# Expert stage of a conv-attention kernel: expert outputs on four rows, 21 weight buffers, outputs gathered group by group, and half of the tokens turned back earlier

## The chip, the cores and the metric

The kernel runs on one core of a Trainium2 chip. Its time is the device time of one execution in microseconds (us); three runs of the kernel before gave 2455.71, 2457.27 and 2457.47, median 2457.27. The profile is of one more execution. Engines: PE multiplies matrices (PEld is its weight load), DVE and ACT are the vector and the scalar engine, POOL a general one, SP issues transfers; ACT can issue transfers too, from its own queue.

## The reference

Four images of 128 channels and 64 x 64 pixels (4096 tokens each) pass a convolution with attention over all pixels (layer 0), then a causal attention over tokens with eight heads, then a layer of 64 experts. In that last part each expert picks its own tokens. In short:

```python
t = t + L1_attn(ln_t(t))                      # B=4, 4096 tokens, D=128
x = ln_t(t)
logits = x @ gate_w.T + gate_b                # B, 4096, E=64
probs = softmax(logits, axis=1)               # over tokens
vals, idx = top_k(probs.transpose(0, 2, 1), 8)      # 8 tokens for each expert and image
pooled = einsum('bked,bke->bed', gathered_x, topv)  # weighted sum of the 8 tokens
h = concat([pooled.transpose(1, 0, 2), 1])
h = gelu(einsum('ebd,edh->ebh', h, weight1))        # 128 -> 512, exact gelu
out = einsum('ebh,eho->ebo', concat([h, 1]), weight2)  # 512 -> 128
outputs[b, idx] += out * topv                 # back to the picked tokens
t = t + outputs                               # then to B, C, H, W
```

An expert thus sees four vectors, one for each image, and has 512 KB of weights.

## The kernel before

Layer 0 and the attention take the first 2288.66 us of the span and are the same in both kernels but for the matmuls with the means and a copy of them on POOL, named below. The tokens `t` stay in SBUF, 128 tokens by 128 channels in each of 128 chunks. A block is 512 tokens (four chunks); there are 32 blocks (`NB`), eight for each image.

**The loop.** `loop()` runs the attention over the 32 blocks. The order of its instructions on PE is as written (`manual_schedule`). Two blocks behind the attention it computes gate logits (`gate_stats`, `gate_norm`, `gate_turn`, `gate_logits`) into `lgs[p]`, where p = 0 holds images 0 and 1 on the two halves of the partitions, and p = 1 images 2 and 3. Once images 0 and 1 are complete, eight rounds of the loop each also pool one of their blocks: `pick_mark` marks each expert's chosen tokens, `pick_exp` takes the exponentials on ACT, `pick_keep` sets all others to zero (so `lgs` becomes a sparse weight for each expert and token), `pick_turn` transposes it and multiplies by the tokens' reciprocal deviation, and `pick_sum` (line 1007) multiplies it with the tokens `t`, and a second time with their means, a matmul of a single column. `pick_add` adds the block's sum to `total`.

**After the loop** the order on each engine is planned by the framework from its own estimates of instruction times and arrivals; an engine then runs its list in order. A tile that is written again waits for its earlier readers. There are four parts:

- Gate of the last block, then `select(1)` (the 8 largest logits of each expert).
- Pooling of images 2 and 3: for each of eight blocks `pick` (mark, exp, keep), `pick_turn`, `pick_sum` into the PSUM tile `pp`. `pool_tokens` subtracts the mean, scales, and transposes into `pooled`, which holds 32 columns for each expert: four images and 28 zeros.
- Experts, in 16 groups of four. `first(g)` (line 1168) multiplies `pooled` with each expert's first weights into `ph`; the four experts use four different column strips of PE and write 32 rows each. ACT copies `ph` to `hr`, `turn` transposes it (`htr`, line 1180), DVE adds the bias (`hs`), ACT applies Gelu. `second(g)` (line 1195) multiplies with the second weights into `po`; DVE adds `po` to `outs`. Weights come on SP's queue into 15 buffers (`load_expert`, line 1117); a buffer is loaded again once `second` has read it. Between groups `back(n)` (line 1209) turns two blocks of `t` back to channels by tokens: four transposes, and one copy on DVE or ACT. One of `lgs`'s blocks is scaled on ACT for each group.
- End: 16 transfers gather the four used rows of `outs` into `eo` (line 1233; half on SP, half on ACT). For each block and image a matmul `sct` (line 1249) spreads the outputs to the tokens, DVE adds it to `t` (line 1256), and SP writes two blocks at a time to memory (line 1259).

PSUM tiles of the tag `kv` after the loop (transposes, logits, `sct`) share four buffers.

Of the kernel before, what the change touches and what calls it, by code (L numbers as in the profile page):

```python
# [18 lines left out]
def conv_attn_hybrid_kernel(  # L19
# [90 lines left out]
    def load_layer1(upper):  # L110
        nc.sync.dma_start(out=wks, in_=wkt.rearrange("d (h e) -> d h e", h=NH))
        nc.sync.dma_start(out=wvs, in_=wvt)

# [554 lines left out]
    NW = 15  # L668

    def layer1(pre, ready):  # L670

        with ExitStack() as kept, ExitStack() as l1:
# [226 lines left out]
            total = lgp.tile([P, B // 2, C + 1], F32, tag="total", name=f"{pre}total")  # L899
# [7 lines left out]
            def gate_norm(n, engine):  # L907
# [9 lines left out]
                nc.gpsimd.tensor_copy(mv1[:, bass.ts(n, CPB), :], gmv[n])  # L917
# [9 lines left out]
            def gate_logits(n, ps):  # L927
# [7 lines left out]
                nc.scalar.activation(lg, pl[rows_b, :], AF.Identity, bias=gbs[rows_b, :])  # L935
# [24 lines left out]
            def pick_mark(p, k):  # L960

                left = gp.tile([P, BLK], F32, tag="left", name=f"{pre}left_{p}_{k}")
# [21 lines left out]
            def pick(p, k):  # L984
                pick_mark(p, k)
                pick_exp(p, k)
                pick_keep(p, k)

# [13 lines left out]
            def pick_sum(p, k, pp, start, stop):  # L1002
                for c in range(CPB):
                    for z in range(2):
                        at = (2 * p + z) * NCH + k * CPB + c
                        for to, what in ((slice(0, C), t[:, at, :]), (slice(C, C + 1), mv1[:, at, 0:1])):
                            nc.tensor.matmul(  # L1007
                                pp[z * E : (z + 1) * E, to], cts[p, k][:, c, z, :], what,
                                start=start and c == 0, stop=stop and c == CPB - 1,
                                skip_group_check=True,  # L1010
                            )

            def pick_add(p, k):
                pp = ps_kv.tile([P, BLK], F32, tag="kv", name=f"{pre}pp_{p}_{k}")[:, : C + 1]
                pick_sum(p, k, pp, True, True)
                if k == 0:
                    nc.vector.tensor_copy(total[:, p, :], pp)
                else:
                    nc.vector.tensor_add(total[:, p, :], total[:, p, :], pp)
# [9 lines left out]
            def loop():  # L1029
# [3 lines left out]
                for n in range(NB):  # L1033
# [18 lines left out]
                    with ExitStack() as order:  # L1052
# [3 lines left out]
                        if 0 <= k0 < NBLK:  # L1056
                            order.enter_context(tc.issue_after(pick_mark(0, k0)))
# [46 lines left out]
            fwp = pool("fw", NW)  # L1104
# [3 lines left out]
            ps_h = pool("l2h", 2, space=PSUM)  # L1108
# [4 lines left out]
            def load_expert(e):  # L1113
                if e >= E:
                    return
                w = fwp.tile([P, FH + FC * C], F32, tag="fw", name=f"{pre}fw_{e}")
# [3 lines left out]

            outs = fo.tile([P, EG, C], F32, tag="outs", name=f"{pre}outs")
            for u in range(QG):
                nc.sync.dma_start(
# [200 lines left out]
```

## Time and profile before

| what | us |
|---|---|
| median of three runs | 2457.27 |
| profiled execution | 2455.56 |
| its span, first to last instruction | 2453.8 |
| end of the loop (`t` written, line 888) | 2288.66 |
| first mark of images 2 and 3 (line 964) | 2300.07 |
| first expert matmul (line 1168) | 2327.50 |
| first `sct` matmul (line 1249) | 2421.56 |
| end of the span | 2453.8 |

Times in the trace count from the first instruction. In a row of the timeline or of the chain the first number is the start and the second the length of what follows; `x4` says how many instructions the row holds. A row of the waits gives who waited for whom: us in total, times, longest. A row of a stage gives its stretch and length, the busy time of PE, PEld, DVE, ACT and POOL with their instruction counts, PE's granted clock (1.00 is full), the DMA engines' mean busy share, and GB/s. A busy PE counts matmuls in flight, whose ends are modelled.

### The profile page before, as it was taken

The numbers are of one execution on the slowest core, as the hardware profiler recorded it, in microseconds if no ns is written. First come the engines' busy times: TensorE is split into PE (matmuls) and PEld (weight loads), VectorE is DVE, ScalarE is ACT, GpSimd is POOL, SyncE is SP. The second block draws the span as 40 slices with busy tenths as digits, with TensorE's granted clock in tenths as the row PEclk, the third lists the DMA queues.
The fourth block names the chain that finished last, engine by engine and source line by source line (L and its number), as shares of the span: only waits on it lengthen the run. The fifth ranks groups of instructions, "written<-read, shape, count | busy, mean of one in ns | idle before, by whom it ended". The sixth has DMA issues, their size and how long they took to land.

```text
span 2453.8 us, 46279 instructions
## 1 busy us (share of the span) xinstructions
PE 2374.9 (97%) x19732; PEld 1584.1 (65%) x19732; DVE 1490.7 (61%) x2619; ACT 1218.0 (50%) x1624; POOL 308.2 (13%) x370
## 2 busy tenths in 40 slices
PE   6999999999999999999999998999999999999797
PEld 3567777677677677777877764555555556555543
DVE  6666666666656666555555556666666766666524
ACT  4454444444443544434434345666666666665341
POOL 0000000000000000000000003333333333334000
PEclk9999999999999999999999999999999999999898
DMA  2200020001200000200000001212121211121495
GB/s 75 79 22 16 20 61 1 18 11 24 65 5 1 22 18 14 61 5 1 1 1 1 1 1 36 54 37 53 37 51 40 48 43 37 37 53 37 165 358 202
DMA packets 60583, 111.08 MB, mean 45 GB/s; under 512 B 10192, under 2 KB 35408, under 8 KB 60240
## 3 DMA queue, kind: packets, MB, share of 16 engines
q1 hardware_dynamic: 58560, 106.53, 14.9%
q8 instruction: 156, 2.56, 0.4%
q10 hardware_dynamic: 1808, 1.51, 0.2%
q14 instruction: 59, 0.48, 0.1%
HBM read 86.38 MB, written 8.91 MB: 39 GB/s over the span
## 4 chain that ended last, share of the span: by engine, by line
PE 93%; DVE 4%; ACT 2%; issue 1%; DMA 0%; SPq 0%; DVEq 0%; ACTq 0%
PE av L510 35%; PE sc L485 18%; PE pk L722 9%; PE pv L840 9%; PE po L876 4%; PE pt L856 2%; PE ps L741 2%; PE ph L1168 1%; PE po L883 1%; PE otr L549 1%; PE pl L931 1%; PE pp L1007 1%; PE pe L427 1%; PE pa L452 1%; PE po L1195 1%; PE otr L1209 1%
## 5 line engine op out<-in xcount | busy, mean ns | idle before, releaser
L510 PE MATMUL av<-pr,am 64*128 64x512 f32 x4096 | 1050.7, 592 | 0.7 <-ACT pr L489 0.7
L489 ACT ACTIVATE pr<-sc 128x1024 f32<-128x1024 f32 x512 | 523.0, 1022 | 671.8 <-PE sc L485 603.0
L492 DVE TENSOR_TENSOR acc<-acc,pr 128x1024 f32<-128x1024 f32 x480 | 586.5, 1222 | 443.7 <-ACT pr L489 443.4
L510 PEld LDWEIGHTS av<-pr,am 64*128 64x128 f32 x4096 | 637.6, 187 | 252.2 <-issue 40.2
L485 PE MATMUL sc<-e,e 64*128 64x512 f32 x2048 | 607.9, 592 | 0.0
L485 PEld LDWEIGHTS sc<-e,e 64*128 64x128 f32 x2048 | 315.5, 187 | 102.7 <-issue 20.0
L722 PE MATMUL pk<-xt,wks 128*128 128x512 f32 x512 | 242.5, 613 | 6.3 <-DVE inside L656 4.2
L840 PE MATMUL pv<-wvs,xt 128*128 128x512 f32 x512 | 226.9, 596 | 2.1 <-ACT v L844 2.1
L844 ACT ACTIVATE v<-pv 128x512 f32<-128x512 f32 x256 | 152.6, 597 | 69.7 <-PE pv L840 69.7
L724 ACT ACTIVATE ks<-pk 128x512 f32<-128x512 f32 x256 | 148.6, 597 | 61.4 <-PE pk L722 61.1
L828 DVE TENSOR_TENSOR em<-em,rb 128x1024 f32<-128x1024 f32 x64 | 80.0, 1251 | 159.9 <-DMA rb<-rd 157.3
L840 PEld LDWEIGHTS pv<-wvs,xt 128*128 128x128 f32 x512 | 97.0, 191 | 121.2 <-issue 115.9
L722 PEld LDWEIGHTS pk<-xt,wks 128*128 128x128 f32 x512 | 91.9, 192 | 113.2 <-issue 81.6
L876 PEld LDWEIGHTS po<-v,em 64*64 64x64 f32 x4096 | 111.4, 133 | 26.7 <-DVE before L866 26.7
L819 POOL TENSOR_TENSOR em<-et,mask 128x1024 f32<-128x1024 f32 x64 | 120.3, 1901 | 8.1 <-ACT et L806 8.1
L96 POOL TENSOR_SCALAR xg<-t,gmv,grs 128x128 f32<-128x128 f32 x120 | 95.3, 806 | 197.4 <-DVE grs L92 141.8
L730 POOL MEMSET ew<- 128x1024 f32 x1 | 1.0, 951 | 942.0 <-PE pa L452 942.0
L876 PE MATMUL po<-v,em 64*64 64x128 f32 x4096 | 119.2, 271 | 0.0
L778 DVE RECIPROCAL rr<-rr 128x512 f32<-128x512 f32 x32 | 107.3, 3353 | 1.1
L763 ACT ACT_TABLE_LOAD x24 | 30.8, 1283 | 118.9 <-DVE ss L762 118.9
L764 POOL COPY state<-mm 128x1 f32<-128x1 f32 x32 | 20.6, 643 | 505.4 <-DVE mm L758 505.3
L866 DVE TENSOR_TENSOR before<-before,pt 128x128 f32<-128x128 f32 x256 | 72.5, 283 | 10.0 <-PE pt L856 4.2
(169 smaller groups left out, 2147.5 us busy)
## 6 DMA issues: line engine op xcount, KB each, us to landing
rb<-rd SPq DMA_DIRECT2D x128, 256.0 KB
fw<-in_fw_dram SPq DMA_DIRECT2D x64, 512.0 KB
t<-in_xtok_dram SPq DMA_DIRECT2D x32, 256.0 KB
out_dram<-t SPq DMA_DIRECT2D x16, 512.0 KB
e<-ee SPq DMA_DIRECT2D x63, 128.0 KB
x<-in_x_dram SPq DMA_DIRECT2D x14, 512.0 KB
e<-ee SPq DMA_DIRECT2D x63, 64.0 KB
x<-in_x_dram ACTq DMA_DIRECT2D x2, 512.0 KB
```

The costliest lines, as they stand in the source:

```text
L96: i = engine.tensor_scalar(out=dst, in0=t[:, chunk, :], scalar1=mean, scalar2=rs, op0=ALU.subtract, op1=ALU.mult)
L485: nc.tensor.matmul(sc[:, u, :], e2[halves[u], p, :], e1[halves[u], :], start=True, stop=True)
L489: nc.scalar.activation(pr, sc, AF.Exp)
L492: added.append(nc.vector.tensor_add(acc, acc, pr).ins)
L510: nc.tensor.matmul(av, am[h, j, :], pr[h, u, :], start=(j == 0), stop=(j == NCH - 1))
L722: nc.tensor.matmul(pk, wks[:, h, :], xt, start=True, stop=True)
L724: nc.scalar.activation(ks, pk, AF.Silu)
L778: inverse = nc.vector.reciprocal(rr, rr).ins
L819: nc.gpsimd.tensor_tensor(em, eq.unsqueeze(2).to_broadcast([P, 2 * NH, H2]), mask.unsqueeze(1).to_broadcast([P, 2 * NH, H2]), ALU.mult,)
L840: nc.tensor.matmul(pv.rearrange("p h d -> p (h d)"), xt[:, bass.ts(2 * q + s, P)], wvs[:, bass.ts(m, BLK)], start=True, stop=True,)
L844: last = nc.scalar.activation(v[:, bass.ts(m, HPB), :], pv, AF.Silu).ins
L876: nc.tensor.matmul(po[s * H2 : (s + 1) * H2, u, q, :], aas[q][half, s, h, :], vs[2 * q + s][half, h, :], start=(q == 0 and h == 0), stop=F ...
```

## The change

- `pick_sum` no longer multiplies with the means. `pool_tokens` takes the mean of the pooled sum over its 128 channels instead, which is the same number. The copy of the means on POOL is gone, and `total` holds images 0 and 1 only; for images 2 and 3 `pool_tokens` reads `pp` itself.
- `pooled` holds four columns for each expert. The matmuls of `first` and `second` have four rows, at the first four of each strip's 32. Two `ph` tiles and one `po` tile with two halves stay for the whole stage; three matmuls with zeros clear them once. `hs` has 4 columns for each expert and chunk instead of 32.
- 21 weight buffers: 19 of the pool, and `wks` and `wvs`, the attention's projections, which nobody needs after the loop (the branch for out-of-range inputs, not taken here, loads them again).
- `outs` is gone. Each group's `po` is copied to `og` (two buffers), and four small transfers, two on SP and two on ACT, gather its rows into `eos`. The second bias is added to `eos` at the end.
- Blocks 0 to 15 (images 0 and 1) are turned back during the last gate and the pooling, with copies on ACT; the others during the experts.
- Marks run one block ahead, and `pick_turn` one block behind. Two tiny activations load the tables of Sqrt and Gelu ahead of their use.
- Outputs leave in steps of 1, 1, 2, 2, 1, 1 blocks instead of two at a time.

```diff
-    NW = 15
+    NW = 21
...
-                nc.gpsimd.tensor_copy(mv1[:, bass.ts(n, CPB), :], gmv[n])
...
-                        for to, what in ((slice(0, C), t[:, at, :]), (slice(C, C + 1), mv1[:, at, 0:1])):
-                            nc.tensor.matmul(
-                                pp[z * E : (z + 1) * E, to], cts[p, k][:, c, z, :], what,
-                                start=start and c == 0, stop=stop and c == CPB - 1,
-                                skip_group_check=True,
-                            )
+                        nc.tensor.matmul(
+                            pp[z * E : (z + 1) * E, :], cts[p, k][:, c, z, :], t[:, at, :],
+                            start=start and c == 0, stop=stop and c == CPB - 1,
+                        )
...
-            fwp = pool("fw", NW)
+            fwp = pool("fw", NW - 2)
             fo = pool("l2fo")
             fs = pool("l2fs", 2)
             ps_a = pool("l2a", 4, space=PSUM)
-            ps_h = pool("l2h", 2, space=PSUM)
+            ps_h = pool("l2h", space=PSUM)
...
+                if e % NW >= NW - 2:
+                    w = wvs if e % NW == NW - 1 else wks.rearrange("d h e -> d (h e)")
+                else:
+                    w = fwp.tile([P, FH + FC * C], F32, tag="fw", name=f"{pre}fw_{e}")
                 nc.sync.dma_start(out=w, in_=fw[e])
                 expert_weights[e] = (w[:, :FH], w[:, FH:].rearrange("p (c o) -> p c o", c=FC))
 
-
-            outs = fo.tile([P, EG, C], F32, tag="outs", name=f"{pre}outs")
-            for u in range(QG):
-                nc.sync.dma_start(
-                    out=outs[u * QW : (u + 1) * QW], in_=fb2[u : u + 1].to_broadcast([QW, EG, C])
-                )
             for e in range(NW):
                 load_expert(e)
 
-
-            pooled = fo.tile([C, E, QW], F32, tag="pooled", name=f"{pre}pooled")
-            nc.gpsimd.memset(pooled, 0.0)
-
+            eos = [fo.tile([P, C], F32, tag=f"eo{p}", name=f"{pre}eo_{p}") for p in range(B // 2)]
+            fb2s = fo.tile([P, C], F32, tag="fb2s", name=f"{pre}fb2s")
+            for z in range(2):
+                nc.scalar.dma_start(out=fb2s[z * E : (z + 1) * E, :], in_=fb2)
+
+
+            pooled = fo.tile([C, E, B], F32, tag="pooled", name=f"{pre}pooled")
+            phs = [ps_h.tile([P, FH], F32, tag=f"ph{i}", name=f"{pre}ph_{i}") for i in range(2)]
+            pos = ps_p.tile([P, 2, C], F32, tag="po", name=f"{pre}po2")
+            zeros = fo.tile([1, P], F32, tag="zeros", name=f"{pre}zeros")
+            nc.gpsimd.memset(zeros, 0.0)
+
+            def back(n, engine):
+
+                ptr = ps_a.tile([P, CPB, P], F32, tag="kv", name=f"{pre}otr_{n}")
+                at = t[:, bass.ts(n, CPB), :]
+                for c in range(CPB):
+                    nc.tensor.transpose(ptr[:, c, :], t[:, n * CPB + c, :], ident)
+                if engine is nc.scalar:
+                    nc.scalar.copy(at, ptr)
+                else:
+                    nc.vector.tensor_copy(at, ptr)
+
+
+            HB = NB // 2
+            turns = list(range(NB))
+
+            def backs(m, engine):
+                for _ in range(m):
+                    back(turns.pop(0), engine)
+
+
+            seed = fs.tile([P, 2], F32, tag="seed", name=f"{pre}seed", bufs=1)
+            with tc.issue_after(copied[pre, NB - 2]):
+                nc.scalar.activation(seed[:, 0:1], eps5, AF.Sqrt)
             gate_stats(NB - 1)
             gate_norm(NB - 1, nc.vector)
+            for to in (*phs, pos.rearrange("p i o -> p (i o)")):
+                nc.tensor.matmul(
+                    to, zeros, ones[0:1, :].to_broadcast([1, to.shape[-1]]), start=True, stop=True
+                )
+            backs(3, nc.scalar)
             gate_turn(NB - 1, ps_a)
+            backs(2, nc.scalar)
             gate_logits(NB - 1, ps_a)()
             select(1)
-            pp = ps_p.tile([P, C + 1], F32, tag="pp", name=f"{pre}pp_1")
+            backs(2, nc.scalar)
+            pp = ps_p.tile([P, C], F32, tag="pp", name=f"{pre}pp_1")
+
+            def mark(k):
+                pick_mark(1, k, fs.tile([P, BLK], F32, tag="hr", name=f"{pre}left_1_{k}"))
+
+            mark(0)
             for k in range(NBLK + 1):
                 if k < NBLK:
-                    pick(1, k)
-                    pick_turn(1, k, ps_a)
+                    exp = pick_exp(1, k)
+                if k + 1 < NBLK:
+                    mark(k + 1)
+                if k < NBLK:
+                    pick_keep(1, k)
                 if k:
+                    pick_turn(1, k - 1, ps_a)
                     pick_sum(1, k - 1, pp, k == 1, k == NBLK)
+                if turns and turns[0] < HB:
+                    backs(1, nc.scalar)
             divisors(1)

             def pool_tokens(p, sums):
+                mean = fs.tile([P, 2], F32, tag="mean", name=f"{pre}mean_{p}", bufs=1)
+                nc.vector.tensor_reduce(mean[:, 0:1], sums, AX.X, ALU.add)
+                nc.vector.tensor_scalar_mul(mean[:, 1:2], mean[:, 0:1], 1.0 / C)
                 row = fs.tile([P, C], F32, tag="row", name=f"{pre}row_{p}", bufs=1)
                 nc.vector.tensor_scalar(
-                    out=row, in0=sums[:, :C], scalar1=sums[:, C : C + 1],
+                    out=row, in0=sums, scalar1=mean[:, 1:2],
                     scalar2=rden[:, p : p + 1], op0=ALU.subtract, op1=ALU.mult,
...
-            pool_tokens(0, total[:, 0, :])
-            nc.vector.tensor_copy(total[:, 1, :], pp)
-            pool_tokens(1, total[:, 1, :])
+            pool_tokens(0, total)
+            pool_tokens(1, pp)
 
             def first(g):
 
-                ph = ps_h.tile([P, FH], F32, tag="ph", name=f"{pre}ph_{g}")
+                ph = phs[g % 2]
                 for u in range(QG):
                     e = g * QG + u
                     nc.tensor.matmul(
-                        ph[u * QW : (u + 1) * QW, :], pooled[:, e, :], expert_weights[e][0],
+                        ph[u * QW : u * QW + B, :], pooled[:, e, :], expert_weights[e][0],
                         start=True, stop=True,
...
-                hs = fs.tile([P, FC, QG, QW], F32, tag="hs", name=f"{pre}hs_{g}")
+                hs = fs.tile([P, FC, QG, B], F32, tag="hs", name=f"{pre}hs_{g}")
                 nc.vector.tensor_tensor(
-                    hs, ptr,
+                    hs, ptr[:, :, :, :B],
                     fb1s[:, bass.ts(g, QG), :].rearrange("p u c -> p c u")
-                    .unsqueeze(3).to_broadcast([P, FC, QG, QW]), ALU.add,
+                    .unsqueeze(3).to_broadcast([P, FC, QG, B]), ALU.add,
                 )
                 return hs, nc.scalar.activation(hs, hs, AF.Gelu).ins
 
             def second(g, hs):
-                po = ps_p.tile([P, C], F32, tag="po", name=f"{pre}po2_{g}")
+                po = pos[:, g % 2, :]
                 for c in range(FC):
                     for u in range(QG):
                         nc.tensor.matmul(
-                            po[u * QW : (u + 1) * QW, :], hs[:, c, u, :],
+                            po[u * QW : u * QW + B, :], hs[:, c, u, :],
                             expert_weights[g * QG + u][1][:, c, :],
                             start=(c == 0), stop=(c == FC - 1),
                         )
+                og = fs.tile([P, C], F32, tag="og", name=f"{pre}og_{g}")
+                nc.vector.tensor_copy(og, po)
                 for u in range(QG):
                     load_expert(g * QG + u + NW)
-                nc.vector.tensor_add(outs[:, g, :], outs[:, g, :], po)
-
-            def back(n):
-
-                ptr = ps_a.tile([P, CPB, P], F32, tag="kv", name=f"{pre}otr_{n}")
-                at = t[:, bass.ts(n, CPB), :]
-                for c in range(CPB):
-                    nc.tensor.transpose(ptr[:, c, :], t[:, n * CPB + c, :], ident)
-                if n % 2:
-                    nc.scalar.copy(at, ptr)
-                else:
-                    nc.vector.tensor_copy(at, ptr)
-
+                by = og.rearrange("(u w) o -> w u o", u=QG)
+                for p in range(B // 2):
+                    for z in range(2):
+                        at = z * E + g * QG
+                        (nc.scalar if p else nc.sync).dma_start(
+                            out=eos[p][at : at + QG, :], in_=by[2 * p + z]
+                        )
+
+            with tc.issue_after(exp):
+                nc.scalar.activation(seed[:, 1:2], eps5, AF.Gelu)
             hr = first(0)
             for g in range(EG):
                 hs, gelu = turn(g, hr)
                 if g + 1 < EG:
                     hr = first(g + 1)
-                for n in range(g * NB // EG, (g + 1) * NB // EG):
-                    back(n)
+                if turns:
+                    backs(1, nc.vector)
+                if turns and g % 2 and g < EG - 2:
+                    backs(1, nc.scalar)
                 p, k = g // NBLK, g % NBLK
                 probs = lgs[p][:, bass.ts(k, BLK)]
                 with tc.issue_after(gelu):
                     nc.scalar.activation(probs, probs, AF.Copy, scale=rden[:, p : p + 1])
                 second(g, hs)
-            eo = []
+            backs(len(turns), nc.vector)
+            for eo in eos:
+                nc.vector.tensor_add(eo, eo, fb2s)
+
             for p in range(B // 2):
-                eo_p = fo.tile([P, C], F32, tag=f"eo{p}", name=f"{pre}eo_{p}")
-                for z in range(2):
-                    for u in range(QG):
-                        row = u * QW + 2 * p + z
-                        (nc.scalar if p else nc.sync).dma_start(
-                            out=eo_p[z * E : (z + 1) * E, :].rearrange("(g u) o -> u g o", u=QG)[u],
-                            in_=outs[row : row + 1],
-                        )
-                eo.append(eo_p)
-
-            OB = 2
-            for p in range(B // 2):
-                for k0 in range(0, NBLK, OB):
+
+                for k0, OB in ((0, 1), (1, 1), (2, 2), (4, 2), (6, 1), (7, 1)):
```

## The prediction

> **What bounds the kernel now.** I read the page's span and chain first, then busy time by stage, then the chain in order of time inside the last stages, then the waits of SP's queue.
>
> ```profile
> span 2453.8 us, 46279 instructions
> PE 93%; DVE 4%; ACT 2%; issue 1%; DMA 0%; SPq 0%; DVEq 0%; ACTq 0%
> ...
> 2288.66:2300.07 11.41, 3.23 (x6) 1.23 (x6) 5.30 (x24) 4.13 (x5) 2.18 (x3) 0.68 1.02 318
> 2300.07:2327.50 27.43, 22.20 (x290) 18.56 (x290) 17.89 (x38) 6.51 (x16) 0.00 (x0) 0.82 0.49 195
> 2353.00:2417.60 64.60, 55.12 (x568) 28.95 (x564) 17.62 (x34) 26.06 (x44) 0.00 (x0) 1.00 0.76 295
> 2417.60:2453.80 36.20, 22.48 (x64) 9.90 (x64) 19.48 (x32) 0.00 (x0) 0.00 (x0) 0.76 0.61 238
> ```
>
> PE holds the chain, but the stages differ (columns: stretch, length, busy PE, PEld, DVE, ACT, POOL, then clock, DMA share, GB/s). The loop over token blocks ends at 2288.66. Gate and selection (11.4 us) leave PE idle. Pooling (27.4 us) runs PE at 81%, partly at a reduced clock. Experts run from 2327.50 to 2417.60, the end alone has no ACT work. All that the change touches lies in the last 165 us, but for one matmul pair inside the loop.
>
> One group of four experts, from the chain in order of time:
>
> ```profile
> 2396.07 0.66 PE htr L1180 x4
> 2396.73 0.44 PE otr L1209 x4
> 2397.16 0.98 PE ph L1168 x2
> 2398.14 0.59 PE otr L1209 x4
> 2400.66 0.65 PE ph L1168 x2
> 2401.39 0.59 ACT hr L1173
> 2402.03 0.66 PE htr L1180 x4
> ...
> SPq L1117 <- PE po L1195: 71.2, 13, 29.5
> ```
>
> A group takes 5.96 us (2396.07 to 2402.03). It is PE's written order, with one gap: the last ph ends, ACT copies hr, htr starts 0.77 us later. No wait of PE on weights appears; SP, on the contrary, waits for po to free weight buffers (last line).
>
> **The change, part by part.** Sums are made against the span, 2453.8. The profiled execution took 2455.56; the median of the runs is 2457.27, 3.5 above the span, and I carry that over.
>
> *1. Mean column of pooling, in the loop.* Each of 8 loop rounds loses 16 one-column matmuls.
>
> ```profile
> 2155.07 0.45 PE L1007 MATMUL pp<-t,ct 128*64 128x128 f32 x4
> 2155.42 0.44 PE L1007 MATMUL pp<-t,ct 128*64 128x128 f32 x4
> 2164.57 0.85 PEld L883 LDWEIGHTS po<-before,rr 128*64 128x64 f32 x16 [0.17 <-issue]
> ```
>
> A quarter of pp with its means takes 0.34 us, so 1.34 a round; 16 matmuls of the same shape without means take 0.85 (L883). Rounds with pooling last 26.7 us (t written at 1984.10 and 2010.83), rounds without 24.95, all PE: 8 x 0.49 = **-3.9**. POOL's copy of the means goes too (0.19 us, beside idle POOL: nothing).
>
> *2. Gate to first mark.* Sqrt's table load moves ahead of the wait it stood behind:
>
> ```profile
> 2290.68 1.28 ACT L91 ACT_TABLE_LOAD   x1 [6.05 <-DVE gmv L88]
> 2293.02 1.15 PE L923 MATMUL gtr<-ident,xg 128*128 128x128 f32 x4 [4.43 <-DVE xg L96]
> 2294.90 2.08 PE L931 MATMUL pl<-xt,gws 128*128 128x512 f32 x2 [0.73 <-ACT xt L925]
> ```
>
> That is -1.28. Turned blocks and three zeroing matmuls (estimate 0.43 + 2 x 0.85, from ph's 0.43 a pass) fill PE's idle 4.4 us, so pl should run at full clock, 1.04 for 2.08. They also stand before gtr on PE, and five copies stand before xt and lg on ACT: +0.7. **-1.6**; the first mark starts at 2298.5. If the gate's own work waits for them longer, the bound is 0. The bias loads on ACT (2 x 0.63) and the seeds lie in ACT's 6 us of idle.
>
> *3. Pooling.* Now each block goes mark, exp, keep, turn, multiply, sum, and takes up to 3.2 us; from 2300.07 to the last pp at 2325.97 it is 25.9. With marks a block ahead, DVE's 0.79 + 0.71 + 0.62 (starts of mark, keep and ct, one after another) is 2.12 a block, 17.0 for eight. Added: the first exp (0.5), and at the end PE's order, in which ctr of block 7 stands behind two pp and a turned block (about 2.0), then multiply 0.6 and pp 0.9. About 21, and 0.6 more for a slow clock at first: 21.6, **-4.3**. The turned blocks' copies (16 x 0.58 in all) go to ACT, which is busy for 6.5 of 27.4 us here; without that room each would hold up an exp by 0.6. Mean and scaling (0.29 like the copy that goes, then 0.15) add **+0.2**. So ph of group 0 starts 5.7 us earlier than before within this stage and the last.
>
> Here a rule speaks against the change. The Trainium skill, *TensorE: Matmul & The Clock Gate*, Part 4, says that transposes do not count as PE activity for the clock, and half of what PE now does here is transposes.
>
> ```profile
> 2306.36:2309.77 3.41, 3.41 (x41) 3.12 (x40) 2.04 (x4) 0.98 (x4) 0.00 (x0) 0.50 1.03 412
> 2412.17:2415.58 3.41, 2.54 (x23) 1.39 (x15) 1.16 (x3) 0.74 (x2) 0.00 (x0) 1.00 0.00 0
> 2415.58:2419.00 3.42, 1.08 (x32) 0.81 (x32) 0.70 (x2) 1.57 (x3) 0.00 (x0) 1.00 0.01 2
> ```
>
> In stretches of 3.41 us, full clock came back only after one wholly busy (first line). But the second line kept it with ordinary matmuls only until 2413.17, 1.0 us, and 1.5 us of transposes, while the third, with 1.08 us of matmuls, lost it. So the row says that transposes count, at least to keep the clock. By the row 21.6; by the rule PE stays at half clock and is the bound: (0.43 + 0.43 + 0.86) x 2 = 3.4 a block, 27.5 and 3.6 around it, 31. I take the row and keep the rule for the range.
>
> *4. Experts.* PE's order in the built program, for a late group: htr, first ph of the next group, po of two groups ago, the other three ph together, htr. With the chain's rows: 0.50 + 0.98 + 0.93 (po with 32 matmuls took 1.01 before a full-array matmul) + 1.03 + 0.77 = **4.21**. It falls because po no longer has a ph between its first two matmuls; four rows in place of 32 change no streaming time of PE. hs shrinks to an eighth on DVE and ACT (0.69 and 0.63, estimate 0.2 and 0.25), off PE's path. Sixteen of 32 turned blocks have moved to stages 2 and 3; 15 of the others fall between htr of groups 1 and 15, 0.5 each. Fourteen steps: 14 x 4.21 + 7.5 = 66.4; less 4 x 0.77 where the early order covers the copy of hr, less two po and one ph that fall elsewhere (2.9): **60.4**. Before them 5.9: first ph to first po end, 7.55 before, less Gelu's table load of 1.28 and a smaller hs. After them: two po 1.9; og, two gathers on ACT (0.63 each) before the last Gelu, po 1.0, og 0.3, two more pairs of gathers and their landing. Last gather's issue began at 2421.98 before and landed at 2424.09, 2.1. That is 8.1. Sum 5.9 + 60.4 + 8.1 = **74.4** against 94.1 (2327.50 to 2421.56): **-19.7**.
>
> Weights: 21 of 64 are in place before group 0 (19 from one stream, two earlier). wks is loaded ahead of the last rd and rb on SP, but needs only the last keys, done 20 us before rr. The reload of both in the branch that doesn't run costs nothing. The 43 others start at 5.9 and take 1.28 each (0.524 MB at 410 GB/s, seen at 2306): 55.0, landing 2, one gap 1: 64 after first ph. The last ph needs them at 64.5. So weights are at par with PE: a cover of 0.5 us, and each us lost in the stream is then a us of span.
>
> The gathers are new waits. On SP a pair stands behind four loads and waits for og; behind it stand the next loads, for which ph waits three to five groups later. og has two buffers, so og of group g waits for the gather of g-2, on DVE, with hs behind it; hs has two groups to spare. On ACT a pair (1.26) stands between hr and the next Gelu. A busy ACT has 3.3 us of work in 4.21. Four gathers of 2 KB beside 2 MB are nothing in bytes, and before, 8 issues in 4.99 us overlapped in flight.
>
> *5. End.* The 16 gathers of outs are gone, counted above. Output:
>
> ```profile
> 2417.62 5.27 ACTq L1233 DMA_DIRECT2D eo<-outs  x8
> 2421.56 2.04 PE L1249 MATMUL sct<-lg,eo 64*128 64x512 f32 x2 [4.37 <-DMA eo<-outs]
> 2427.51 19.15 SPq L1259 DMA_DIRECT2D out_dram<-t  x16
> ```
>
> From first sct to the end it is 32.2, of which output's 8.39 MB at 408 GB/s is 20.6. The first transfer now leaves after one block (2.9, not 5.95), but PE has idled about 4 us and blocks come at 1.7 us at half clock for four blocks, so the stream starves. I take **-1.7**, between 0 and -3.
>
> Sum: -3.9 - 1.6 - 4.3 + 0.2 - 19.7 - 1.7 = **-31.0**. Span 2422.8; median 2457.27 - 31.0 = **2426.3**.
>
> **Rivals.** *The clock stays at half through pooling* (the rule above): +9.4, 2435.7. *Gathers hold up PE*: ACT issues a pair before Gelu and the next hr; if og is late by its buffers, hr is late by up to 1.26 a step, eleven steps, +7 to +14: 2433 to 2440. For it: the weight stream is at par, so SP runs behind; against it: po lags two groups. *Better overlap*: full clock throughout pooling (-1) and at the end (-3), output stream never starved, hr's gap covered in more steps (5 x 0.77): 2418. *Slower*: a gather in the weights' queue stops the stream until it has landed. A group's stream is then 5.1 + 2 x 2.1 = 9.3, and 10.75 groups take 100, with 18 around them 118 against 74.4: 2470. It decides from 8.1 us a group, where the gain is gone. Against it is the overlap of eight gathers above. *No effect*: weights and PE order as before; excluded by the order read in the build.
>
> **How the numbers follow.** Main case 0.53 (own range 2420 to 2432), clock 0.15, gathers 0.15, better overlap 0.13, stream stopped 0.03, unchanged 0.01. The range, 2415 to 2440, holds the first four but for their edges. 0.2% (4.9 us) is about what measurement of this kernel can tell. Faster 0.95, same 0.02, slower 0.03.
>
> **What would show it.** Loop rounds with pooling at 26.2 us; no table load between gmv and grs; first ph 9.6 us earlier; late steps htr to htr near 4.2; no wait of ph on weights before group 14; first output transfer 3 us after the first sct. Wrong if pooling's clock is 0.5 to its end, if steps lengthen to 5 us or more, or if DVE's og waits for DMA.

## The result, and the profile after

The changed kernel takes 2434.07 us (median of 4 runs, 2431.80 to 2438.91) where the kernel before, on the same chip, takes 2456.57 (2455.71 to 2457.47): ratio 0.9911, 95% interval 0.9894 to 0.9928. So it is 22.5 us faster; 31.0 were predicted. The profiled execution took 2434.62, its span is 2432.9.

First the page's span and the busy time by stage, cut at the same events as before: the loop's end, the first mark, the first ph, the first sct, the end (columns as in the prediction: stretch, length, busy PE, PEld, DVE, ACT, POOL, then clock, DMA share, GB/s).

```profile
span 2432.9 us, 45864 instructions
...
2285.59:2296.76 11.17, 9.39 (x44) 6.45 (x43) 5.30 (x23) 6.63 (x12) 0.19 (x1) 0.85 0.89 340
2296.76:2320.33 23.57, 19.37 (x194) 16.58 (x194) 17.49 (x39) 12.62 (x27) 0.00 (x0) 0.86 0.61 242
2320.33:2402.94 82.61, 68.84 (x768) 29.99 (x769) 15.67 (x45) 25.01 (x53) 0.00 (x0) 1.00 0.76 276
2402.94:2432.90 29.96, 19.82 (x64) 10.53 (x64) 19.60 (x33) 0.00 (x0) 0.00 (x0) 0.81 0.74 283
```

Gate 11.17 (11.41 before), pooling 23.57 (27.43), experts 82.61 (94.06), end 29.96 (32.24). The experts give the largest part, and they are also where the gain falls short: 11.5 of 19.7 us.

One late group in time order (start, length, engine, line, instruction, and in brackets the idle time before it and what ended it):

```profile
2355.94 0.66 PE L1226 MATMUL htr<-ident,hr 128*128 128x128 f32 x4 [1.01 <-ACT hr L1219]
...
2356.43 0.60 PE L1141 MATMUL otr<-ident,t 128*128 128x128 f32 x4
...
2357.07 0.69 DVE L1145 COPY t<-otr 128x512 f32<-128x512 f32 x1 [2.56 <-PE otr L1141]
2357.68 0.28 DVE L1247 COPY og<-po 128x128 f32<-128x128 f32 x1
...
2358.01 1.06 PE L1241 MATMUL po<-fw,hs 128*4 128x128 f32 x32
...
2359.28 0.22 DVE L1230 TENSOR_TENSOR hs<-htr,fb1s 128x64 f32<-128x64 f32 x1 [1.33 <-PE po L1241]
2359.54 0.26 ACT L1235 ACTIVATE hs<-hs 128x64 f32<-128x64 f32 x1 [3.65 <-DVE hs L1230]
...
2360.93 0.66 PE L1226 MATMUL htr<-ident,hr 128*128 128x128 f32 x4 [1.01 <-ACT hr L1219]
```

A step is 4.99 us, with two turned blocks 5.48. Read as a chain it goes round through four engines: otr, its copy on DVE, og behind that copy, po (it waits for og), hs (it waits for po), Gelu, then 0.70 of scaling, hr, htr. From 2366 the steps get longer (5.86, 5.09, 5.73, 6.30, 5.63), and the waits change. The waits of the expert stage (waiter, line, what it waited for: us in all, times, longest):

```profile
DVE og L1247 <- DMA eo<-og: 12.6, 6, 3.2
...
PEld ph L1214 <- DMA fw<-in_fw_dram: 7.3, 7, 1.2
...
PE ph L1214 <- DMA fw<-in_fw_dram: 0.9, 4, 0.3
```

The waits of SP's queue, from 2320 to 2400:

```profile
SPq L1118 <- DMA fw<-in_fw_dram: 23.8, 27, 2.0
SPq L1118 <- PE po L1241: 22.4, 1, 22.4
SPq L1118 <- DMA eo<-og: 4.0, 2, 2.0
```

And the traffic over the same 80 us, in slices of 2 us:

```profile
GB/s 0 0 0 121 292 338 299 243 387 356 323 343 420 394 372 399 341 322 397 410 393 291 299 327 393 411 336 320 320 360 416 389 369 330 315 316 32 3 10 5
```

PE now waits for weights, which it never did before, and og waits for gathers. Before, nearly all of SP's waiting was for po; now it waits for po once, before the first loads, and from there on for its own transfers. Once the stream runs, from 2342 on, it is at 290 to 420 GB/s (mean of the slices some 365 up to 2366 and 357 from there to 2390), not at a steady 410. From the first load at 2326.22 to the end of the last ph's wait at 2393.26 are 67.0 us for 43 loads, 1.56 each.

### The profile page after: what moved, and what is told of

It is laid out like the page before. It is cut to its first block, busy times and chain, and to the rows that moved or that the text cites. A ratio compares the mean times of both kernels' runs of the same rounds, so it can differ in the third digit from the quotient of the medians.

```text
span 2432.9 us, 45864 instructions
## 1 busy us (share of the span) xinstructions
PE 2360.8 (97%) x19482; PEld 1569.3 (65%) x19482; DVE 1504.9 (62%) x2619; ACT 1213.7 (50%) x1631; POOL 304.1 (13%) x338
```

## The experiments

All stage lengths below come from the profile of each kernel, in us. "Loop" runs from the seventeenth of the 32 additions to t that end a round to the last of them; "last ph" is the first of the two passes that multiply with the last expert's first weights, counted from the first ph. "Median" is of the timed runs (a single run where one is marked). The sets were timed beside the kernel before, whose median was 2456.57 with the change, 2455.96 with gathers_pool, po_two, both and no_gather, 2455.39 with best, nw15, late_turns and mean_loop, 2455.81 with best2, gathers_act and gate_first, and 2456.52 (one run) with half_sp; medians of different sets are comparable only to about 1 us.

| kernel | before that | loop | gate | pooling | experts | last ph | end | span | median |
|---|---|---|---|---|---|---|---|---|---|
| before | 1907.8 | 380.9 | 11.41 | 27.43 | 94.06 | 84.65 | 32.24 | 2453.8 | 2456.57 |
| after | 1906.6 | 379.0 | 11.17 | 23.57 | 82.61 | 72.93 | 29.96 | 2432.9 | 2434.07 |
| gathers_pool | 1907.6 | 379.3 | 9.67 | 22.29 | 76.85 | 68.60 | 32.70 | 2428.4 | 2432.18 |
| po_two | 1906.3 | 381.9 | 11.14 | 22.18 | 81.15 | 72.26 | 30.76 | 2433.4 | 2435.41 |
| both | 1909.3 | 379.1 | 9.67 | 22.40 | 77.91 | 69.39 | 31.53 | 2429.9 | 2429.42 |
| no_gather | 1909.8 | 379.3 | 9.67 | 22.30 | 72.36 | 67.07 | 30.41 | 2423.8 | 2425.30 |
| best | 1908.9 | 379.1 | 9.67 | 22.38 | 78.35 | 68.21 | 30.90 | 2429.2 | 2431.76 |
| nw15 | 1907.3 | 378.4 | 11.46 | 23.48 | 87.75 | 80.55 | 30.82 | 2439.2 | 2442.94 |
| late_turns | 1910.1 | 380.6 | 10.13 | 20.57 | 84.95 | 75.07 | 30.37 | 2436.7 | 2433.80 |
| mean_loop | 1907.8 | 383.0 | 9.68 | 22.18 | 82.02 | 72.35 | 31.58 | 2436.2 | 2438.07 |
| best2 | 1910.2 | 379.3 | 9.67 | 22.23 | 75.23 | 67.61 | 30.38 | 2427.0 | 2429.80 |
| gathers_act | 1909.9 | 379.3 | 9.67 | 22.18 | 96.55 | 86.29 | 31.62 | 2449.2 | 2451.47 (1 run) |
| gate_first | 1907.8 | 379.2 | 10.36 | 25.03 | 82.77 | 73.07 | 30.36 | 2435.6 | 2437.38 (1 run) |
| half_sp | 1909.7 | 379.4 | 9.67 | 22.32 | 77.97 | 67.89 | 31.00 | 2430.0 | 2431.71 (1 run) |

The part ahead of everything that was edited varies from 1906.3 to 1910.2 between single profiles. That is why small effects are read here from stages, and from medians only where several runs stand behind them.

One thing changes beside each edit. The framework plans PE's order anew for every kernel. In the change, po_two, late_turns, mean_loop, gate_first and half_sp a group's po comes mostly in one piece, and two or three of them stand behind the last htr. In gathers_pool, both, no_gather, best, best2 and gathers_act only one does, and from the seventh group on the matmuls of po and of ph alternate; nw15 lies between. A difference between the two kinds is therefore not the edit's alone.

Two theories stood against each other for the experts' missing 8.2 us. S: the stream of weights, which the gathers slow. R: the ring between DVE and PE shown above.

### Gathers on another queue (gathers_pool)

```diff
-                        (nc.scalar if p else nc.sync).dma_start(
+                        nc.gpsimd.dma_start(
```

> All four gathers of a group are issued on POOL's queue; SP issues only weights, ACT only its own work. Theory S (the weight stream): the gathers in SP's queue, and the completion semaphores they share with the loads, are what made 43 loads take 67 us (first issue to last landing) where 57 were expected. Then the last weights land 64 to 66 us after the first ph instead of 72.9, PE no longer waits for fw, and first ph to first sct falls from 82.6 to about 78; median about 2429.5, where the rest is set by the loop between DVE and PE. Theory R (the ring: po waits for og, og stands behind a turned block on DVE, hs waits for po): steps from htr to htr stay at 4.99 and 5.48 with turned blocks whatever the stream does, and only the last four steps get shorter; between -1 and -4.6. If neither gathers nor their queue matter: 2434.

Measured: experts 76.85, 5.8 less than after; the last ph starts at 68.6, not 72.9, and the last weights land 67.0 us after the first ph, a little later than the 64 to 66 of theory S. The stage's list of waits, PEld's included, has no line for fw any more, and the traffic from 2320 to 2400 reads:

```profile
GB/s 0 0 33 269 298 332 374 419 412 402 399 407 408 391 395 401 410 391 409 405 393 410 397 414 404 400 411 405 399 400 403 333 58 10 1 7 5 7 8 117
...
eo<-og POOLq DMA_DIRECT2D x64, 2.0 KB, 5.0
```

The same weights now come at about 400 GB/s from 2334 on. The second line is the median time of a gather from issue to landing, 5.0 us. The landings kept in the trace of the change give 4.3 for the same gathers on SP's and ACT's queues (median of all 64), and 1.6 to 2.1 for those that were issued once the stream had ended: most of the 5.0 is the stream's, not the queue's. The way from the last htr to the first sct is 6.5 us, against 7.9 in the change and 3.5 without gathers; PE's order has a part in these three. The later steps are 4.98 and 5.88 with one and two turned blocks and 4.65 without. So far S holds; half_sp, below, shows it with PE's order unchanged. The median, 2432.18, is only 1.9 below the change's, and the two intervals overlap; the profile's end stage was 2.7 longer at a lower clock (0.76 for 0.81), which goes against part of the 5.8.

### Two banks for po (po_two), and both edits

```diff
+            pob = ps_p.tile([P, C], F32, tag="pp", name=f"{pre}pob")
+            nc.vector.memset(pob, 0.0)
...
-                po = pos[:, g % 2, :]
+                po = pob if g % 2 else pos[:, 0, :]
```

> po alternates between two PSUM tiles (the second takes over the bank of pp), so that po of a group no longer waits for og of the group before. Theory R: steps of htr in the middle groups fall from 4.99 and 5.48 to 4.2 to 4.7. Theory S: the weights then bind earlier, PE waits for fw from about group 8 instead of 12, first ph to first sct stays at 82 to 83, and the time within 1 us of 2434. If R alone set the time, 2427 to 2429.

Measured: experts 81.15, median 2435.41. The ring is open: hs no longer waits for po. But the middle steps fall from 4.99 and 5.48 only to 4.79 and 5.28, as PE's order shows:

```profile
2356.18 0.66 PE L1229 MATMUL htr<-ident,hr 128*128 128x128 f32 x4 [0.80 <-ACT hr L1222]
2356.68 0.60 PE L1141 MATMUL otr<-ident,t 128*128 128x128 f32 x4
2357.21 1.02 PE L1217 MATMUL ph<-fw,pooled 128*4 128x512 f32 x2
2358.26 1.06 PE L1244 MATMUL pob<-fw,hs 128*4 128x128 f32 x32
2359.14 1.04 PE L1217 MATMUL ph<-fw,pooled 128*4 128x512 f32 x6
2360.97 0.66 PE L1229 MATMUL htr<-ident,hr 128*128 128x128 f32 x4 [0.80 <-ACT hr L1222]
```

That is 0.50 + 0.53 + 1.05 + 0.88 + 1.83 from start to start, PE without a gap but for hr's 0.80. The prediction had 4.21 + 0.5 = 4.71 for such a step. So the ring cost 0.2 us a step, and what it gave came back as waits for weights: late steps of 6.15, 5.09, 6.62, 5.08 and 6.31. R as the main cause falls.

The diff of "both" is the two together.

> Both edits: gathers on POOL's queue and po in two tiles. Theory S with R as the second limit: first ph to first sct at 73 to 76, the 74.4 of the prediction, and 2425 to 2428. Theory S alone would give no more than gathers_pool, R alone no more than po_two.

Measured: experts 77.91, median 2429.42. In the stage there is no gain over gathers_pool (76.85). The expectation of 73 to 76 was missed: with the stream free, the ring wasn't the second limit either. (The steps are those of gathers_pool, 4.98, 5.88 and 4.65.)

### No gathers (no_gather)

```diff
-                by = og.rearrange("(u w) o -> w u o", u=QG)
-                for p in range(B // 2):
-                    for z in range(2):
-                        ...
+                if g == EG - 1:
+                    for p in range(B // 2):
+                        nc.vector.tensor_copy(eos[p], og)
```

> The gathers are left out (eo is filled from the last group's og by two copies on DVE), so the output is not the experts'. It bounds what the gathers cost in all. Theory S: the stream as in gathers_pool, last weights at 64 to 66 after first ph, and at the end about 2 us less for the landing of the last gather: 2427 to 2428. If the loads are slow for another reason (late release by PE), still 70 or more after first ph, and 2432.

Measured: experts 72.36, median 2425.30. Without the gathers the stage is 10.2 us shorter: 5.9 up to the last ph (72.9 to 67.1) and 4.4 after it (9.7 to 5.3). Part of the latter is PE's order: behind the last htr stand three po in the change and one here. The late steps without turned blocks are 4.65 here too, where the prediction had 4.21: PE takes po and ph in turns in this build, which the prediction's order did not have.

### Which gathers: only ACT's queue (gathers_act), only SP's pair (half_sp)

```diff
-                        (nc.scalar if p else nc.sync).dma_start(
+                        nc.scalar.dma_start(
```

> All four gathers of a group on ACT's queue, SP issues loads only. It tells the place in SP's queue from what gathers and loads share elsewhere (the completion semaphores, the DMA engines). If SP's queue is the cause: no wait of PE for weights, stretches of 10 us at 400 GB/s and over. If the shared semaphores are: loads still wait for the fourth load before them and for gathers, stretches at 340 to 370 GB/s as in the change. Either way ACT carries 2 issues more a group (1.0 to 1.3 us), steps of 5.5 or more, first ph to first sct 82 to 90.

Measured: experts 96.55, longer than in the kernel before (94.06) and beyond the 82 to 90 that were expected. SP's queue holds loads alone, and yet (waits of SP from 2320 to 2400, then of ACT in the whole stage):

```profile
SPq L1118 <- DMA eo<-og: 26.8, 11, 6.0
```
```profile
ACT hr L1219 <- DMA eo<-og: 36.2, 8, 5.8
```

Loads wait 26.8 us for gathers of another queue, and hr, a copy on ACT, stands 36.2 us behind gathers that wait for earlier transfers to land. What ties them is seen in the built program: every transfer of SP and ACT is given one of eight completion semaphores, and it waits until the last transfer on that semaphore has landed. In the changed kernel a late stretch of SP's queue is

```
L1254 eo<-og  [waits DMAHW0, DVE]
L1254 eo<-og  [waits DMAHW1]
L1118 fw<-in_fw_dram  [waits DMAHW2, PE]
L1118 fw<-in_fw_dram  [waits DMAHW3, PE]
L1118 fw<-in_fw_dram  [waits DMAHW6, PE]
L1118 fw<-in_fw_dram  [waits DMAHW7, PE]
```

and ACT's pair has 4 and 5. So each load waits for the fourth load before it: four in flight at most. In gathers_pool the loads go round over all eight. The traces keep the landings of every semaphore, and from these the loads in flight can be counted:

| kernel | loads in flight, mean of 2342 to 2382 (most) | one load, issue to landing (median, us) | first issue to last landing, us a load |
|---|---|---|---|
| gathers_act | 2.9 (4) | 5.3 | 1.76 |
| after | 3.9 (4) | 5.7 | 1.56 |
| half_sp | 5.3 (6) | 7.4 | 1.44 |
| gathers_pool | 7.6 (8) | 10.4 | 1.42 |
| no_gather | 7.8 (8) | 10.2 | 1.42 |

In the change the count stands at its limit of four nearly all the time, so what holds the stream there is the limit and not a lack of free buffers. From five on, more in flight gives next to nothing.

half_sp leaves ACT's pair out and keeps SP's.

```diff
-                for p in range(B // 2):
+                if g == EG - 1:
+                    nc.vector.tensor_copy(eos[1], og)
+                for p in range(1):
```

> Only SP's pair of gathers a group is kept, ACT's pair is left out (its half of eo is filled once from the last group's og, so that half of the output is not the experts'). It parts the two pairs. In the built program eight completion semaphores go round over all transfers of SP and ACT: in the change the gathers take four and the loads have four, here the loads come round over all eight, with two gathers between four loads. If SP's own pair, in the loads' queue, is what slows the stream: first ph to first sct 79 to 82, stretches at 340 to 370 GB/s. If the semaphores that ACT's pair takes, and the loads' waits on them, are: 73 to 76, at 390 GB/s and over.

Measured: last ph at 67.9, 0.8 later than without any gather (67.1), and the traffic from 2320 to 2420 in slices of 2.5 us:

```profile
GB/s 0 0 7 211 247 375 420 414 397 411 390 413 370 395 375 393 377 405 361 406 400 408 408 413 398 408 264 9 7 5 6 0 0 309 206 400 400 380 383 410
```

With two gathers between every four loads in SP's own queue the stream keeps to about 400 GB/s. It is only just enough: PEld still waits 5.3 us for fw, in the last groups. The stage as a whole, 77.97, lies between the two expectations, because the way from the last htr to the first sct stays long (8.3 us; 7.9 in the change, with the same three po behind that htr). PE's order in the late groups is nearly the change's, so this is the cleanest of the comparisons: ACT's pair accounts for 5.0 of the 5.9 us up to the last ph. It left three things with it: two semaphores of the eight, two issues a group on ACT, and half of what og waits for. gathers_act and the count of loads in flight speak for the semaphores: had the other two held up the stream by freeing buffers later, fewer than four loads would be in flight. (The loads' waits for loads do not: they are 23.8 us in the change and 28.9 in no_gather, where the stream is full and they cost nothing.) No run changed the number of semaphores alone, and to that extent it stays open.

### A kernel from this (best, best2)

```diff
-                        (nc.scalar if p else nc.sync).dma_start(
+                        (nc.gpsimd if g < EG - 2 else nc.scalar if p else nc.sync).dma_start(
...
-                og = fs.tile([P, C], F32, tag="og", name=f"{pre}og_{g}")
+                og = fs.tile([P, C], F32, tag="og", name=f"{pre}og_{g}", bufs=4)
```

> Gathers of groups 0 to 13 on POOL's queue, those of the last two groups, when no load is left, on SP's and ACT's as in the change (a gather on POOL's queue takes 5.0 us from issue to landing, one on SP's or ACT's 2), and og with four buffers instead of two. If the stream is what the gathers held up: first ph to first sct at 73 to 75 (76.9 with all gathers on POOL's queue, 72.4 without gathers), 2425 to 2428. If the landing of the last gather is hidden and og's buffers cost nothing: the 76.9 stays, and 2430 to 2432.

Measured: experts 78.35, median 2431.76. The expectation was missed. ACT's queue had group 14's pair ahead of the last hr, and the last step took 6.36 us. best2 gives ACT only the last group's pair.

```diff
-                        (nc.gpsimd if g < EG - 2 else nc.scalar if p else nc.sync).dma_start(
+                        (nc.gpsimd if g < EG - 2 else nc.scalar if p and g == EG - 1 else nc.sync).dma_start(
```

> As the kernel with four og buffers and the last two groups off POOL's queue, but the gathers of group 14 all on SP's queue: on ACT's they stood ahead of the last hr and made the last step 6.36 us instead of 4.65. First ph to first sct 78.35 less about 2: 76, so 2427 to 2430. If the last hr waits for something else: 78, 2431.

Measured: experts 75.23, median 2429.80 (2426.28 to 2431.60), ratio to before 0.9892, interval 0.9876 to 0.9909. The stage is 7.4 us shorter than the change's, the median 4.3 (3.5 if each is taken against the kernel before of its own set). It is the fastest complete kernel here beside "both" (2429.42); its interval and the change's overlap.

### Single parts of the change undone

nw15 has the weight buffers of before.

```diff
-    NW = 21
+    NW = 15
```

> 15 weight buffers as before the change, all else as changed (13 from the pool, wks and wvs). Six more loads come after the first ph. If the stream at 1.56 us a load (67 us for 43) sets the experts' end: last weights at about 82 us after first ph instead of 72.9, first ph to first sct 91 to 93, and +8 to +10: 2442 to 2444. At 1.28 a load +7.7. If PE or DVE set it: 2434 to 2436.

Measured: median 2442.94, 8.9 more than after; the last ph starts 7.6 us later, 1.27 for each of the six loads. The experts' stage grew by 5.1 only (87.75, where 91 to 93 were expected), because the way after the last ph got shorter: in this build one po stands behind the last htr. Of the change's parts that were undone here, the buffers are worth most.

late_turns puts the sixteen turned blocks of the first half back into the expert stage.

```diff
-            backs(3, nc.scalar)
             gate_turn(NB - 1, ps_a)
-            backs(2, nc.scalar)
             gate_logits(NB - 1, ps_a)()
             select(1)
-            backs(2, nc.scalar)
...
-                if turns and turns[0] < HB:
-                    backs(1, nc.scalar)
...
-                if turns and g % 2 and g < EG - 2:
+                if turns:
                     backs(1, nc.scalar)
```

> The 16 turned blocks of the first half are put back into the expert stage (two a group), gate and pooling keep the three zeroing matmuls only. By the prediction's sum each block costs PE 0.5 us in the expert stage: +8, 2442. If the weight stream sets that stage, PE has the time while it waits: first ph to first sct grows by 0 to 3 only; gate and pooling by -1.5 (less in the way of gtr) to +5 (PE idles and the clock stays at half through pooling): 2434 to 2440.

Measured: median 2433.80, the change's time. Experts 84.95, +2.3 where +8 was the price by the prediction's sum; gate and pooling 30.7, against 34.7 in the profile of after and 32.0 in most others. In the expert stage PE has the time for these blocks while weights come.

mean_loop puts the one-column matmuls back.

```diff
-                        nc.tensor.matmul(
-                            pp[z * E : (z + 1) * E, :], cts[p, k][:, c, z, :], t[:, at, :],
+                        for to, what in ((slice(0, C), t[:, at, :]), (slice(C, C + 1), mv1[:, at, 0:1]))[: 1 + (p == 0)]:
+                            nc.tensor.matmul(
+                                pp[z * E : (z + 1) * E, to], cts[p, k][:, c, z, :], what,
...
```

> The sixteen one-column matmuls a round are put back into the eight loop rounds with pooling (on other one-column data, their sum is not used). By the prediction +3.9; by the profiles, where the eight rounds got shorter by 2.6 in all, +2.6 less what the last round gave back (0.7), between +1.9 and +2.6: 2436 to 2437.

Measured: loop 382.96 against 378.99, +4.0, and median +4.0 (5.2 against the kernel before of each set). The prediction's 3.9 is the right price of the column.

gate_first issues the gate's transpose, logits and selection ahead of the zeroing matmuls and of the seven turned blocks.

```diff
+            gate_turn(NB - 1, ps_a)
+            gate_logits(NB - 1, ps_a)()
+            select(1)
             for to in (*phs, pos.rearrange("p i o -> p (i o)")):
...
-            backs(3, nc.scalar)
-            gate_turn(NB - 1, ps_a)
-            backs(2, nc.scalar)
-            gate_logits(NB - 1, ps_a)()
-            select(1)
-            backs(2, nc.scalar)
+            backs(7, nc.scalar)
```

> The gate's transpose, logits and selection are issued ahead of the zeroing matmuls and the seven turned blocks. By the prediction's step 2 these hold gtr and xt up by 0.7: loop's end to first mark 11.2 down to 9.0 to 10.4. If they keep the clock up instead, pl takes 2.1 instead of 1.1 and the stage stays at 9.7 to 11.4, and pooling, 22.2 to 23.6, gets 1 to 3 longer.

Measured: gate 10.36, pooling 25.03, 35.4 together: longer than with the turned blocks ahead (34.7, and 32.0 in most profiles). In the gate the clock was 0.67, for 0.85 to 1.00. In this one profile the change's place for these blocks is the better one; a single profile does not settle it.

## Why the prediction was nearly right, and where it was short

The direction and the place were right, the size was not: 22.5 us in the medians, and 20.9 in the two spans, of 31.0. By its steps, against the spans:

*1. Mean column.* Predicted -3.9. Taken alone it is worth that (mean_loop, 4.0). The eight rounds with pooling did fall by 4.3 in all, to 26.2 each, as it said. But from before to after the loop fell by 1.9 only (380.9 to 379.0). The round ahead of those with pooling went from 24.73 to 26.44 us and the last round from 17.61 to 18.34; these give back 2.4. The prediction's step costed the matmuls and not what else moves in the loop. What made these two rounds longer was not tested.

*2. Gate.* Predicted -1.6, measured -0.24 in after's profile, and -1.74 (9.67 or 9.68) in eight of the ten other profiles whose gate is not edited. The order of the instructions at this place is the same in both. The difference is the granted clock: eight transposes of turned blocks ahead of gtr took 1.97 us in after, where the stage had 0.85, and 1.09 in gathers_pool, where it had 1.00. No edit accounts for it.

*3. Pooling.* Predicted 27.4 - 4.1 = 23.3, measured 23.57, with the last pp 21.8 us after the first mark (predicted 21.6). Three stretches of 3.41 us of after:

```profile
2299.41:2302.82 3.41, 3.39 (x24) 2.88 (x23) 3.38 (x8) 2.22 (x5) 0.00 (x0) 0.50 1.03 411
2302.82:2306.23 3.41, 3.41 (x25) 3.03 (x23) 2.71 (x6) 2.00 (x5) 0.00 (x0) 0.61 1.03 405
2306.23:2309.65 3.42, 3.42 (x43) 2.91 (x40) 3.42 (x8) 1.26 (x4) 0.00 (x0) 1.00 1.02 410
```

The clock was back some 7 us after dense work began (2299.14), more than half of whose time was transposes, and it stayed. In the gate too: late_turns keeps the three zeroing matmuls there but no turned block, and was granted 0.66, against 0.85 to 1.00 with the blocks. The Trainium skill's statement (*TensorE: Matmul & The Clock Gate*, Part 4) that a transpose does not count as PE activity in the same way would have made pooling 31 us, by the prediction's estimate; for work mixed with ordinary matmuls the measurement decides for the row. Whether transposes alone would do it, no run here shows. The turned blocks there did not pay, though: without them pooling takes 20.57.

*4. Experts.* Predicted 94.1 - 19.7 = 74.4, measured 82.6. This is the step that failed, and of it one term: "The 43 others start at 5.9 and take 1.28 each". They took 1.56 each, and the last ph could start only at 72.9, 8.4 us late, which is the whole miss of the stage. The gathers make up to 5.9 of the 8.4. The other 2.5 are there without any gather: in no_gather the first load lands 4.2 us after its issue, where 2 were set, and the others take 1.36 each. The sentence after it, that each us lost in the stream is a us of span, held roughly: half_sp takes 5.0 off the last ph and 4.6 off the stage, nw15 adds 7.6 and 5.1. The terms beside it were nearer: po first ended 5.9 us after the first ph, as predicted, and a step with a turned block was 4.79 where weights and ring left it alone (po_two), against 4.71. The prediction saw the gathers as waits on DVE and ACT, and as nothing in bytes. It did not see that gathers and loads share completion semaphores: with both pairs, a late group's four gathers take four of the eight, always the same ones, and leave the loads four; with SP's pair alone the loads come round over all eight. That ACT's pair accounts for most of what the gathers cost is measured, and so is the limit of four in flight. That the limit is the way in which this pair slows the stream is the reading that fits best. The rival "gathers hold up PE" named 2433 to 2440, which holds the result; its mechanism, hr late behind ACT's issues because og is late, was there in part only: og did wait for gathers (12.6 us), but the late hr of the last groups waited for ph, and ph for weights.

The -8 for the sixteen turned blocks that left the stage is the same miss seen from PE: a PE that waits for weights has nothing to gain from them. late_turns shows 2.3.

*5. End.* Predicted -1.7, measured -2.3. The first output transfer was issued at 2404.82, 1.9 us after the first sct.

Sum of the misses against the spans: experts 8.2, loop 2.0, gate and pooling 1.6, end -0.6, and -1.2 ahead of the rounds that the table counts as loop, where nothing was edited: 10.0 of the 10.1 us between 31.0 and 20.9.

The marks that the prediction set: steps of 5 us and more, and og waiting for DMA, were named as what would make it wrong. Both came. The first ph came 7.2 us earlier and not 9.6, and ph waited for weights from group 11 on, not from 14.

## What to carry to other kernels

Where a stream of large loads has no slack, small transfers beside it are not costed by bytes or by the time to issue them alone: look up in the built program which completion semaphores they share, and how many large loads are left in flight. When a sum says that two chains end within half a us of each other, removing work from one of them (here, turned blocks from PE) buys little (2.3 us of 8); the first us belongs to the other chain. And an order in which one engine copies for two chains (DVE: turned block, og) should be drawn as a loop before its steps are added, though here it cost only 0.2 us a step.

## What was not expected of the hardware

Loads of 512 KB that keep about 400 GB/s (1.31 us each) with the gathers on POOL's queue, or with SP's pair alone, fell to about 360 when a second pair of 2 KB gathers was on ACT's queue and four loads at most were in flight. Beside the stream a gather of four rows took 4.3 to 5.0 us from issue to landing, whichever queue it was on; after the stream, 1.6 to 2.1 on SP's and ACT's. And the same instructions of gate and pooling took 32.0 or 34.7 us in different executions, with granted clocks of 1.00 and 0.92, or 0.85 and 0.86: single profiles cannot settle an edit worth 2 us there.
